# Reordering an attention block: four heads scored together, units by query tile, and a share of the normalisation on GpSimd

## The chip, the cores and the metric

The kernel runs on one core of a Trainium2 chip. Its time is the device time of one execution in microseconds (us); the median of several runs counts. TensorE (PE) multiplies matrices, and its weight loads have a row of their own (PEld). VectorE is DVE, ScalarE is ACT, GpSimd is POOL, and SyncE (SP) issues most transfers. Each engine works through its instructions in program order and waits for the others by semaphores. All data is float32.

## The reference, cut to what matters

The reference passes 8 sequences of 512 tokens with 128 features through four layers, each a half feed-forward, an attention and again a half feed-forward. Only the last layer, L3, is touched. It computes:

```
x = x + 0.5 * ffn(layernorm(x))
x = x + attention(layernorm(x))
x = x + 0.5 * ffn(layernorm(x))

attention:  q, k, v = x Wq' + bq, x Wk' + bk, x Wv' + bv     # 16 heads of 8 features
            s = q k' / sqrt(8)
            p = softmax(softmax(s))                          # twice
            h = p v
ffn:        probs = softmax(x gate'); the two largest of 8 experts are chosen
            y = sum over the two chosen of (x w_up[e]) w_down[e]
```

## The kernel before, in words

The kernel goes through the layers as blocks: L0, L1, L2 and, last, `l3_block` (L1212). The tensor `self.x[b]` of each of the 8 batches stays on the chip as four tiles of 128 tokens (128 partitions x 4 x 128).

**A unit of L3 attention.** A unit is a batch b, a group g of four heads and a tile i of 128 queries (L1316): 128 units, with i as the innermost index. The four heads of a group lie on four groups of 32 partitions, so that a score product uses a quarter of TensorE's rows. A unit goes through these steps:
- `score(n, h)` (L1238): for the head pair h, two products of 128 queries by 512 keys into one double bank of PSUM, tag `s1`, of which there are two.
- `maximum` (L1246): VectorE takes the negated row maximum of both heads (L1248).
- `soften` (L1250): two exponentials on ScalarE with the row sum (L1255).
- `norm` (L1258): the reciprocal of the sums and a multiply of each head's 128x512 probabilities; VectorE does it (L1268) but for the fourth head in every second unit, which ScalarE does (L1266).
- `turn` (L1270): four transposes a head on TensorE into a bank of tag `tp` (L1276), so that keys lie on the partitions.
- `again` (L1280): the second softmax's exponential out of that bank (L1284). No maximum is needed, as its input lies between 0 and 1.
- `weigh` (L1287): 16 products with the values into bank `o`; a column of ones in the values gives the second softmax's sum. After the last tile of a group ScalarE copies the bank out (L1301).
- `back` (L1304): four transposes, the reciprocal and the multiply of the second softmax, once per batch and group; after a batch's last group, VectorE adds the result to `self.x[b]` (L1314).

**The order.** L1341 to L1370 write the order of PE, ACT and DVE by hand: an iteration n issues pieces of unit n (scores, maxima, exponentials), n-1 (normalisation, turns, second exponential) and n-2 (`weigh`). The score of the first head pair is issued at the end of the iteration before, and the pairs stand apart from each other.

**Other work between the units.** `self.plan` puts steps of other work at given iterations into `todo`, and an iteration runs its list just before `weigh`. This work is, for each batch, the entry of the attention (`whiten`, the layer norm, with `measure` L160: VectorE's statistics, thirteen small GpSimd operations, then one GpSimd operation L197 per tile; `turned` L228: four transposes and a ScalarE copy; `project` L1704 twice and `values` L1718) and the closing feed-forward (`l3_ffn_steps` L266: whiten, turned, route, choose, choose_next, then eight `apply` steps, each a product for four experts and four updates of x on VectorE, L297). Each `project` writes its result to memory and reads it back by four transfers in another layout, all issued on SP. A product of this other work uses the same three `tp` banks as the turns. The last batch's feed-forward begins at iteration 131 and runs after all units; the store of x follows its last `apply`.

Of the kernel before, what the change touches and what calls it, by code (L numbers as in the profile page):

```python
# [108 lines left out]
class Net:  # L109
    def __init__(self, ctx, tc, a, x_in, out):  # L110
# [17 lines left out]
        self.brief = ctx.enter_context(tc.tile_pool(name="brief", bufs=2))  # L128
        self.front = ctx.enter_context(tc.tile_pool(name="front", bufs=2))
# [30 lines left out]
    def measure(self, srcs, bias=False):  # L160
# [3 lines left out]
        n = 4 * len(srcs)  # L164
        st = small.tile([P, n, 6], F32, tag=f"bst{n}", name="st")
        for k, src in enumerate(srcs):
            for i in range(4):
                nc.vector.bn_stats(st[:, 4 * k + i, :], src[:, i, :])  # L168

        sm, d, q, ve, r0, h, rs = (small.tile([P, n], F32, tag=f"b{t}{n}", name=t) for t in ("sm", "d", "q", "ve", "r0", "h", "rs"))  # L170
# [20 lines left out]
    def whiten(self, b, out=None, src=None):  # L191

        src = self.x[b] if src is None else src
        sm, rs = self.measure([src])
        xn = self.act.tile([P, 4, P], F32, tag="xn", name="xn") if out is None else out
        for i in range(4):
            self.nc.gpsimd.tensor_scalar(xn[:, i, :], src[:, i, :], sm[:, i : i + 1], rs[:, i : i + 1], ALU.subtract, ALU.mult)  # L197
        return xn
# [29 lines left out]
    def turned(self, xn, bank, out=None):  # L228

        nc = self.nc  # L230
        pt = bank("pt")
        for i in range(4):
            nc.tensor.transpose(pt[:, i * P : (i + 1) * P], xn[:, i, :], self.ident)
        xt = self.act.tile([P, 512], F32, tag="xt", name="xt") if out is None else out
        nc.scalar.copy(xt, pt)
        return xt

# [28 lines left out]
    def l3_ffn_steps(self, b, w, bank, done=None):  # L266
# [3 lines left out]
        box = {}  # L270

        def route(xt):
            lp = bank("lp", (P, 4, 8))
            for i in range(4):
                nc.tensor.matmul(lp[:, i, :], lhsT=xt[:, i * P : (i + 1) * P], rhs=gw, start=True, stop=True)
            box["steps"] = self.top2_steps(small, lp, 4, None, "b")
            return xt, box["steps"][0](None)
# [5 lines left out]
        def choose_next(got):  # L283
            xt, found = got
            _, o1, o2 = box["steps"][2](found)
            sel = small.tile([P, 4, 8], F32, tag="bsel", name="sel")
# [4 lines left out]
        def apply(got, i, h):  # L291
# [3 lines left out]
            for e in range(4):  # L295
                x = self.x[b][:, i, :]
                nc.vector.scalar_tensor_tensor(x, yp[:, e, :], sel[:, i, 4 * h + e : 4 * h + e + 1], x, ALU.mult, ALU.add)  # L297
            if done is not None and i == 3 and h == 1:
                done(b)
            return got  # L300

        experts = [lambda got, i=i, h=h: apply(got, i, h) for i in range(4) for h in range(2)]
        return [lambda _: self.whiten(b), lambda xn: self.turned(xn, bank), route, choose, choose_next] + experts

    def first_max(self, pool, v, n, tag, oh=None):

        nc = self.nc
        m = pool.tile([P, n], F32, tag=tag + "m", name=tag + "m")
        nc.vector.tensor_reduce(m, v, AX.X, ALU.max)
        r = pool.tile([P, n, 8], F32, tag=tag + "r", name=tag + "r")  # L310
        nc.vector.tensor_tensor(r, v, bc(m, 2, 8), ALU.is_equal)
        nc.vector.tensor_tensor(r, r, bc(self.const("rev"), 1, n), ALU.mult)
        f = pool.tile([P, n], F32, tag=tag + "f", name=tag + "f")
        nc.vector.tensor_reduce(f, r, AX.X, ALU.max)
        oh = pool.tile([P, n, 8], F32, tag=tag + "o", name=tag + "o") if oh is None else oh
# [3 lines left out]
    def top2_steps(self, pool, lp, n, bias, tag, to=(None, None, None)):  # L319
# [3 lines left out]
        def powers(_):  # L323
            lg = pool.tile([P, n, 8], F32, tag=tag + "lg", name="lg")
# [4 lines left out]
            m = pool.tile([P, n], F32, tag=tag + "lm", name="lm")  # L329
            nc.vector.tensor_reduce(m, lg, AX.X, ALU.max)  # L330
            nc.vector.tensor_tensor(lg, lg, bc(m, 2, 8), ALU.subtract)
            pr = pool.tile([P, n, 8], F32, tag=tag + "pr", name="pr") if to[0] is None else to[0]
# [3 lines left out]
        def largest(pr):  # L336
            s = pool.tile([P, n], F32, tag=tag + "ls", name="ls")
# [5 lines left out]
        def next_largest(got):  # L343
            pr, o1 = got
            p2 = pool.tile([P, n, 8], F32, tag=tag + "p2", name="p2")
# [866 lines left out]
    def l3_block(self, w2, w3, out):  # L1212
# [11 lines left out]
        with ExitStack() as c:  # L1224
# [6 lines left out]
            def bank(name, shape=(P, 512)):  # L1231
                return ps.tile(list(shape), F32, tag="tp", name=name, bufs=3)

            scores, maxima, rcs, probs, expos, outs, ats = {}, {}, {}, {}, {}, {}, {}

            def score(n, h):  # L1238
                b, g, i = units[n]
# [10 lines left out]
            def soften(n, h):  # L1250
                s, nm = scores.pop((n, h)), maxima.pop((n, h))
                sm = rcs[n, h] = wk.tile([P, 2], F32, tag="sm", name="sm", bufs=4)
                for jj in range(2):
                    e = wk.tile([P, 512], F32, tag="e", name="e", bufs=14)
# [3 lines left out]
            def norm(n, h):  # L1258

                rc = wk.tile([P, 2], F32, tag="rs", name="rs", bufs=4)  # L1260
                nc.vector.reciprocal(rc, rcs[n, h])
                rcs[n, h] = rc
                for jj in range(2):
                    e = probs[n][2 * h + jj]
                    if h and jj and n % 2:
                        nc.scalar.activation(e, e, AF.Copy, scale=rc[:, 1:2])  # L1266
                    else:
                        nc.vector.tensor_scalar(e, e, rc[:, jj : jj + 1], None, ALU.mult)  # L1268

            def turn(n, h):  # L1270

                banks = []
                for j in (2 * h, 2 * h + 1):
                    tp = bank("tp", (P, 4, P))
                    for kt in range(4):
                        nc.tensor.transpose(tp[:, kt, :], probs[n][j][:, kt * P : (kt + 1) * P], self.ident)  # L1276
                    banks.append(tp)
                return banks

            def again(n, banks):  # L1280

                for tp in banks:
                    p = wk.tile([P, 4, P], F32, tag="p2", name="p2", bufs=10)
                    nc.scalar.activation(p, tp, AF.Exp)  # L1284
                    expos.setdefault(n, []).append(p)

            def weigh(n):  # L1287
                b, g, i = units[n]
                if i == 0:
                    outs[b, g] = ps.tile([P, 512], F32, tag="o", name="o")  # L1290
                    if g == 0:
                        ats[b] = wk.tile([P, 4, P], F32, tag="at", name="at")
                o, p2 = outs[b, g], expos.pop(n)
                for kt in range(4):
                    for j in range(4):
                        nc.tensor.matmul(  # L1296
                            o[32 * j : 32 * j + 32, i * P : (i + 1) * P], lhsT=vas[b % 2][:, kt, 4 * g + j, :], rhs=p2[j][:, kt, :],
                            start=(kt == 0), stop=(kt == 3))
                if i == 3:
                    os = wk.tile([P, 512], F32, tag="os", name="os")  # L1300
                    nc.scalar.copy(os, o)  # L1301
                    outs[b, g] = os

            def back(b, g):  # L1304
                os = outs.pop((b, g))
                tp = bank("tp", (P, 4, 4, 32))
                for i in range(4):
                    nc.tensor.transpose(tp[:, i].rearrange("p j r -> p (j r)"), os[:, i * P : (i + 1) * P], self.ident)
                rc = wk.tile([P, 4, 4], F32, tag="rc", name="rc")
                nc.vector.reciprocal(rc, tp[:, :, :, 8])  # L1310
                nc.vector.tensor_tensor(
                    ats[b][:, :, 32 * g : 32 * g + 32].rearrange("p i (j d) -> p i j d", d=8), tp[:, :, :, 0:8], bc(rc, 3, 8), ALU.mult)
                if g == 3:
                    nc.vector.tensor_tensor(self.x[b], self.x[b], ats[b], ALU.add)  # L1314

            units = [(b, g, i) for b in range(NB) for g in range(4) for i in range(4)]  # L1316
# [8 lines left out]

            self.plan(todo, (0, 2, 3), *self.l2_ffn_steps(NB - 1, w2, bank))
            self.plan(todo, (4, *range(6, 18)), *self.l3_ffn_steps(NB - 1, w3, bank))
            for b in range(NB):
                if b:
                    n = 16 * b - 10  # L1330
                    self.plan(todo, (n, n + 2, n + 3, n + 4, n + 5), lambda _, b=b: self.whiten(b), lambda xn: self.turned(xn, bank, self.longer()),
                              lambda xt, b=b: l3.project(b, 0, xt, bank), lambda xt, b=b: l3.project(b, 1, xt, bank),
                              lambda xt, b=b: l3.values(b, xt, bank))
                for g in range(4):
                    also(16 * b + 4 * g + 6, back, b, g)
                n = 16 * b + 19
                self.plan(todo, (n, *range(n + 2, n + 14)), *self.l3_ffn_steps(b, w3, bank, store))
# [3 lines left out]
            with tc.manual_schedule(engines={mybir.EngineType.PE, mybir.EngineType.Activation, mybir.EngineType.DVE}):  # L1341
                for n in range(last + 20):
                    here, prev, two = 0 <= n < last, 0 <= n - 1 < last, 0 <= n - 2 < last
                    if n == 0:
                        score(0, 0)
                    if prev:
                        banks = turn(n - 1, 0)
                        again(n - 1, banks)
                    if here:
                        maximum(n, 0)  # L1350
                        score(n, 1)
                        soften(n, 0)
                    if prev:
                        norm(n - 1, 1)
                    if here:
                        maximum(n, 1)
                    for work in todo.pop(n, ()):
                        work()
                    if two:
                        weigh(n - 2)  # L1360
                    if prev:
                        banks = turn(n - 1, 1)
                    if here:
                        soften(n, 1)
                    if prev:
                        again(n - 1, banks)
                    if here:
                        norm(n, 0)
                        if n + 1 < last:
# [439 lines left out]
```

## Time and profile before

| | |
|---|---|
| median of 3 runs | 2884.49 us (2880.66 to 2885.62) |
| the profiled execution | 2895.91 us, its span 2894.1 us |
| busy: PE, DVE, ACT, POOL | 2610.5, 1920.7, 1738.7, 904.5 us |
| mean granted TensorE clock | 0.935 of full speed |
| L3: first score to the end | 2054.8 to 2894.1 us |
| last score of L3 | 2850.0 us |
| last exponential of the first softmax | 2852.6 us |

The busy time of an engine counts compute instructions only. A row of a group of instructions names the line, the engine, the operation, what is written and read, the shapes, the count, the busy time in total and the mean duration of one in ns, and last the idle time of the engine just ahead of it with what ended it. A float32 product appears as two matmul records, a transpose as one.

### The profile page before, as it was taken

What the parts mean: (1) busy time and instruction counts of PE and PEld (TensorE: products, weight loads), DVE (VectorE), ACT (ScalarE), POOL (GpSimd) and SP (SyncE); (2) the same over time, 40 slices, a digit from 0 to 9 for tenths busy, and PEclk for the clock granted to TensorE, in tenths of its full rate; (3) what the DMA queues carried; (4) which work ended last, traced back from release to release, by engine and by line L of the source; (5) the groups of instructions that cost most, each with busy time, mean ns of one, the idle gap of its engine ahead of it and who ended that gap; (6) DMA issues with size and microseconds to landing.
All of it is one profiled execution on the core that took longest, in us unless ns stands there. A gap on an engine that the chain in (4) does not pass through costs nothing.

```text
span 2894.1 us, 50615 instructions
## 1 busy us (share of the span) xinstructions
PE 2610.5 (90%) x18466; PEld 1504.0 (52%) x18466; DVE 1920.7 (66%) x5193; ACT 1738.7 (60%) x4258; POOL 904.5 (31%) x1907
## 2 busy tenths in 40 slices
PE   5857766999999998899999999999999999999997
PEld 4545543333333434565655656656555555555553
DVE  5336435788888763546566575654688888888886
ACT  2233133255555555666657566675588888888884
POOL 5744564122223231342524525323312201210200
PEclk9877775799999988999999999999899999999998
DMA  7120340000000000000000000000000000000000
GB/s 250 48 73 16 85 114 16 17 17 17 17 17 17 17 2 32 1 1 1 1 1 1 1 1 1 1 1 15 1 16 16 5 20 16 20 5 20 16 5 8
DMA packets 74343, 67.29 MB, mean 23 GB/s; under 512 B 17760, under 2 KB 63848, under 8 KB 71880
## 3 DMA queue, kind: packets, MB, share of 16 engines
q1 hardware_dynamic: 66128, 51.44, 6.6%
q0 software_dynamic: 3872, 8.11, 1.0%
q10 hardware_dynamic: 4096, 4.51, 0.5%
q8 instruction: 147, 2.41, 0.3%
q14 instruction: 100, 0.82, 0.1%
HBM read 36.74 MB, written 27.33 MB: 22 GB/s over the span
## 4 chain that ended last, share of the span: by engine, by line
PE 65%; DVE 13%; ACT 9%; POOL 8%; issue 3%; DMA 2%; SPq 0%; ACTq 0%; POOLq 0%; DVEq 0%
PE s L1244 8%; PE tp L1276 8%; PE s L1094 5%; PE o L1124 4%; PE o L1538 4%; PE yp L294 4%; PE o L1296 4%; PE s L1489 3%; DVE nm L1095 3%; PE tp L1515 3%; ACT e L1496 3%; PE pp L1458 2%; PE s L1114 2%; PE op L1552 2%; PE vp L1471 2%
## 5 line engine op out<-in xcount | busy, mean ns | idle before, releaser
L171 POOL TENSOR_TENSOR d<-st 128x4 f32<-128x4 f32 (+1 forms) x96 | 19.7, 205 | 1269.2 <-DVE st L168 666.2
L1248 DVE TENSOR_REDUCE nm<-s 128x2 f32<-128x1024 f32 x256 | 313.0, 1223 | 105.4 <-PE s L1244 105.0
L1095 DVE TENSOR_REDUCE nm<-s 128x2 f32<-128x1024 f32 x256 | 307.1, 1219 | 97.4 <-PE s L1114 84.6
L1255 ACT ACTIVATE e<-s,nm 128x512 f32<-128x512 f32 x512 | 351.0, 703 | 29.4 <-DVE nm L1248 29.4
L1116 ACT ACTIVATE pr<-s 128x512 f32<-128x512 f32 x512 | 274.5, 598 | 153.0 <-PE s L1114 144.9
L1114 PE MATMUL s<-q,k 32*128 32x512 f32 x1024 | 312.2, 644 | 10.7 <-ACT pr L1116 6.9
L1284 ACT ACTIVATE p<-tp 128x512 f32<-128x512 f32 x512 | 275.6, 609 | 72.1 <-PE tp L1276 69.9
L1094 PE MATMUL s<-k,q 32*128 32x512 f32 x1024 | 291.0, 672 | 19.0 <-DVE nm L1095 16.3
L1244 PE MATMUL s<-k,q 32*128 32x512 f32 x1024 | 292.0, 648 | 4.8 <-ACT e L1255 2.4
L1276 PE MATMUL tp<-cst,e 128*128 128x128 f32 x2048 | 287.0, 282 | 7.3 <-DVE e L1268 6.2
L1276 PEld LDWEIGHTS tp<-cst,e 128*128 128x128 f32 x2048 | 220.7, 142 | 138.4 <-issue 100.8
L1496 ACT ACTIVATE e<-e,m 128x512 f32<-128x512 f32 (+3 forms) x512 | 285.4, 567 | 7.7 <-DVE m L1493 7.5
L1493 DVE CUSTOM_DVE_ANT_0 e<-s,bias 128x512 f32<-128x512 f32 (+3 forms) x512 | 219.9, 486 | 98.9 <-PE s L1489 98.5
L1517 ACT COPY pt<-tp 128x512 f32<-128x512 f32 x320 | 173.9, 588 | 100.3 <-PE tp L1515 99.8
L1268 DVE TENSOR_SCALAR e<-e,rs 128x512 f32<-128x512 f32 x448 | 201.8, 487 | 9.1
L297 DVE SCALAR_TENSOR_TENSOR x<-yp,sel,x 128x128 f32<-128x128 f32 x512 | 178.5, 349 | 22.6 <-PE yp L294 8.2
L197 POOL TENSOR_SCALAR xn<-x,sm,rs 128x128 f32<-128x128 f32 x228 | 186.0, 827 | 6.1
L1489 PE MATMUL s<-qk 64*128 64x512 f32 (+3 forms) x1024 | 172.7, 456 | 2.3 <-DVE m L1493 1.6
L1515 PE MATMUL tp<-cst,e 128*128 128x128 f32 x1280 | 169.5, 279 | 1.7 <-ACT e L1496 1.7
L1515 PEld LDWEIGHTS tp<-cst,e 128*128 128x128 f32 x1280 | 141.7, 143 | 41.6 <-issue 16.4
L1546 DVE TENSOR_TENSOR att<-o,rt 128x512 f32<-128x512 f32 x64 | 44.3, 692 | 174.7 <-ACT rt L1545 174.7
L1524 POOL COPY rb<-rc 128x512 f32<-128x512 f32 x64 | 39.1, 611 | 383.9 <-DVE rc L1522 311.0
(394 smaller groups left out, 4904.2 us busy)
## 6 DMA issues: line engine op xcount, KB each, us to landing
yd<-z SPq DMA_DIRECT2D x8, 1024.0 KB
r<-yd SPq DMA_DIRECT2D x32, 256.0 KB
xd<-xn SPq DMA_DIRECT2D x16, 256.0 KB
k<-sk SPq DMA_DIRECT2D x64, 64.0 KB
sk<-pu SPq DMA_DIRECT2D x16, 256.0 KB
w<-in_l_w SPq DMA_DIRECT2D x14, 256.0 KB
q<-sq SPq DMA_DIRECT2D x32, 72.0 KB
x<-in_x SPq DMA_DIRECT2D x8, 256.0 KB
```

What stands on the lines that cost most here:

```text
L1094: nc.tensor.matmul(s[:, jj, :], lhsT=q[cut, g, i * P : (i + 1) * P], rhs=k[cut, g, :], start=True, stop=True)
L1095: nc.vector.tensor_reduce(nms[b, g // 2][:, i, 2 * h : 2 * h + 2, g % 2], s, AX.X, ALU.max, negate=True)
L1114: nc.tensor.matmul(s, lhsT=k[cut, g, kt * P : (kt + 1) * P], rhs=q[cut, g, :], start=True, stop=True)
L1116: nc.scalar.activation(e, s, AF.Exp)
L1244: nc.tensor.matmul(s[:, jj, :], lhsT=q[cut, g, i * P : (i + 1) * P], rhs=k[cut, g, :], start=True, stop=True)
L1248: nc.vector.tensor_reduce(nm, scores[n, h], AX.X, ALU.max, negate=True)
L1255: nc.scalar.activation(e, s[:, jj, :], AF.Exp, bias=nm[:, jj : jj + 1], accum_out=sm[:, jj : jj + 1])
L1276: nc.tensor.transpose(tp[:, kt, :], probs[n][j][:, kt * P : (kt + 1) * P], self.ident)
L1284: nc.scalar.activation(p, tp, AF.Exp)
L1489: nc.tensor.matmul(s[:, jj, 0:w], lhsT=qs[n][cut, i * P : (i + 1) * P], rhs=ks[n][cut, 0:w], start=True, stop=True)
L1496: outs.append(lambda e=e, jj=jj: nc.scalar.activation(e, e, AF.Exp, bias=mins[n][:, jj, i : i + 1], scale=-1.0, accum_out=sums[n][:, jj, i ...
L1515: nc.tensor.transpose(tp[:, k, :], block(n, jj, i, kt), self.ident)
```

## The change

1. A unit is now (b, i, g): the head group is the innermost index, so that one query tile is complete after four units. `back` works on one tile for all 16 heads and GpSimd adds it to that tile of x.
2. Both score pairs are issued together at the head of the iteration. Turns move later: heads 0 and 1 of unit n-1 are turned at the end of iteration n, heads 2 and 3 at the head of iteration n+1, between the second exponentials of heads 0 and 1, in two `tp` banks.
3. Other products have one bank of their own, tag `w`; after the last unit, the two double banks of the scores.
4. ScalarE normalises no more; GpSimd normalises the fourth head of each unit from unit 14 on.
5. ScalarE operations of the other work are collected in `self.late` and issued after `soften(n, 0)` or at the end of the iteration. The transfers of `project` are put off with them. The router's exponential is not collected.
6. Other work has new iterations, some in a second place (n + 0.5) after `weigh`; whitening goes tile by tile; GpSimd, too, is in the order written by hand.
7. The last batch's feed-forward is done for tiles 0 to 2 and for tile 3 separately, the first from iteration 127 on.
8. `e` has 12 buffers for 14, `p2` 8 for 10. The helpers take fewer than four tiles.

```diff
@@ turned, scalar
-        xt = self.act.tile([P, 512], F32, tag="xt", name="xt") if out is None else out
-        nc.scalar.copy(xt, pt)
+        xt = self.act.tile([P, 512], F32, tag="xt", name="xt")[:, 0 : n * P] if out is None else out
+        self.scalar(xt, pt, AF.Copy)
         return xt
+
+    def scalar(self, *args, **kwargs):
+
+        work = lambda: self.nc.scalar.activation(*args, **kwargs)
+        if self.late is None:
+            work()
+        else:
+            self.late.append(work)
@@ l3_block
-                return ps.tile(list(shape), F32, tag="tp", name=name, bufs=3)
+                n = int(np.prod(shape[1:]))
+                t = ps.tile([P, 512] if spare[0]["tag"] == "w" else [P, 1024], F32, name=name, **spare[0])[:, 0:n]
+                return t if len(shape) == 2 else t.rearrange("p (a b) -> p a b", b=shape[2])
+
+            turned, spare = dict(tag="tp", bufs=2), [dict(tag="w", bufs=1)]
...
-                    if h and jj and n % 2:
-                        nc.scalar.activation(e, e, AF.Copy, scale=rc[:, 1:2])
-                    else:
-                        nc.vector.tensor_scalar(e, e, rc[:, jj : jj + 1], None, ALU.mult)
...
+                    (nc.gpsimd if h and jj and n >= 14 else nc.vector).tensor_scalar(e, e, rc[:, jj : jj + 1], None, ALU.mult)
+
+            def turn(n, j):
+
+                tp = ps.tile([P, 4, P], F32, name="tp", **turned)
+                for kt in range(4):
+                    nc.tensor.transpose(tp[:, kt, :], probs[n][j][:, kt * P : (kt + 1) * P], self.ident)
+                turns.setdefault(n, []).append(tp)
...
+            def back(b, i):
+                os = outs.pop((b, i))
+                tp = bank("tp", (P, 16, 32))
+                for g in range(4):
+                    nc.tensor.transpose(tp[:, 4 * g : 4 * g + 4].rearrange("p j r -> p (j r)"), os[:, g * P : (g + 1) * P], self.ident)
+                rc, at = wk.tile([P, 16], F32, tag="rc", name="rc"), wk.tile([P, 16, 8], F32, tag="at", name="at")
+                nc.vector.reciprocal(rc, tp[:, :, 8])
+                nc.vector.tensor_tensor(at, tp[:, :, 0:8], bc(rc, 2, 8), ALU.mult)
+                x = self.x[b][:, i, :]
+                nc.gpsimd.tensor_tensor(x, x, at.rearrange("p h d -> p (h d)"), ALU.add)
+
+            units = [(b, i, g) for b in range(NB) for i in range(4) for g in range(4)]
...
             self.plan(todo, (0, 2, 3), *self.l2_ffn_steps(NB - 1, w2, bank))
-            self.plan(todo, (4, *range(6, 18)), *self.l3_ffn_steps(NB - 1, w3, bank))
+            self.plan(todo, (6, 7, 8, 9, 10, 12, 13, 14, 14.5, 15, 16, 17, 19, 20, 21, 22.5, 25.5), *whiten(NB - 1), *self.l3_ffn_steps(NB - 1, w3, bank)[1:])
             for b in range(NB):
+                n = 16 * b
                 if b:
-                    n = 16 * b - 10
-                    self.plan(todo, (n, n + 2, n + 3, n + 4, n + 5), lambda _, b=b: self.whiten(b), lambda xn: self.turned(xn, bank, self.longer()),
+                    m = max(n - 20, 1)
+                    self.plan(todo, (m, m + 1, m + 2, m + 3, m + 4, n - 9, n - 7.5, n - 5, n - 4.5), *whiten(b), lambda xn: self.turned(xn, bank, self.longer()),
                               lambda xt, b=b: l3.project(b, 0, xt, bank), lambda xt, b=b: l3.project(b, 1, xt, bank),
                               lambda xt, b=b: l3.values(b, xt, bank))
...
+                for i in range(4):
+                    also(n + 4 * i + 6, back, b, i)
+                if b < NB - 1:
+                    last_ones = (23, 24, 24.5, 25, 25, 27, 28, 29, 31, 32, 32.5, 33)
+                    self.plan(todo, [n + k for k in (19, 20, 21, 22, 23, *(last_ones if b == NB - 2 else (24, 25, 26, 27, 28, 29, 31, 32, 33, 35, 36, 37)))],
+                              *whiten(b), *self.l3_ffn_steps(b, w3, bank, store)[1:])
+                else:
+                    self.plan(todo, (n + 19, n + 20, n + 20.5, n + 21, n + 21.5, n + 22, n + 22.5), *self.l3_ffn_steps(b, w3, bank, store, (3, 4)))
+                    self.plan(todo, [n + k for k in (15, 16.5, 17, 17.5, 18, 19, 19.5, 20, 20.5, 20.5, 21)], *self.l3_ffn_steps(b, w3, bank, None, (0, 3)))
...
-            with tc.manual_schedule(engines={mybir.EngineType.PE, mybir.EngineType.Activation, mybir.EngineType.DVE}):
+            with tc.manual_schedule(engines={*FIXED, mybir.EngineType.Pool}):
                 for n in range(last + 20):
                     here, prev, two = 0 <= n < last, 0 <= n - 1 < last, 0 <= n - 2 < last
...
+                    if n == last:
+                        spare[0] = dict(tag="s1", bufs=2)
+                    if here:
+                        score(n, 0)
+                        score(n, 1)
+                    if two:
+                        for j in range(4):
+                            again(n - 2)
+                            if j < 2:
+                                turn(n - 2, 2 + j)
                     if here:
                         maximum(n, 0)
...
+                        maximum(n, 1)
                     if prev:
                         norm(n - 1, 1)
+                    works(n)
                     if here:
...
+                        soften(n, 0)
+                    put_off()
                     if two:
                         weigh(n - 2)
+                    works(n + 0.5)
                     if prev:
...
+                        turn(n - 1, 0)
+                        turn(n - 1, 1)
                     if here:
                         soften(n, 1)
...
                         norm(n, 0)
...
+                    put_off()
                 assert not todo
```

## The prediction

> **What bounds the kernel now.** I read the times first: the profiled execution took 2895.91 us (span 2894.1), 0.4% above the 2884.49 us median, so a sum made against it is scaled by 0.9961 at the end. Only the L3 block (2054.8 us to the end) changes. A table of busy time by stretch (us, then busy time of PE, PEld, DVE, ACT, POOL, then the granted clock) shows its limit:
>
> ```profile
> 2400.00:2500.00 100.00, 99.25 (x961) 57.65 (x958) 84.38 (x191) 86.18 (x210) 15.29 (x38) 1.00 0.06 15
> 2850.00:2894.00 44.00, 25.50 (x160) 12.67 (x156) 22.80 (x74) 8.17 (x19) 6.43 (x17) 0.78 0.04 12
> ```
>
> TensorE is full at full clock, here as in every hundred from 2100 to 2800; VectorE and ScalarE are at 85%. The groups of 2100 to 2840 us say how long a unit takes and of what it is made:
>
> ```profile
> L1255 ACT ACTIVATE e<-s,nm 128x512 f32<-128x512 f32 x475 | 325.7, 703 | 11.2 <-DVE nm L1248 11.2
> L1248 DVE TENSOR_REDUCE nm<-s 128x2 f32<-128x1024 f32 x238 | 291.0, 1223 | 90.2 <-PE s L1244 89.8
> L1244 PE MATMUL s<-k,q 32*128 32x512 f32 x952 | 268.2, 640 | 0.0
> L1284 ACT ACTIVATE p<-tp 128x512 f32<-128x512 f32 x476 | 256.0, 609 | 62.9 <-PE tp L1276 60.9 <-ACT p L1284 0.3
> L1268 DVE TENSOR_SCALAR e<-e,rs 128x512 f32<-128x512 f32 x417 | 187.8, 487 | 8.5
> L197 POOL TENSOR_SCALAR xn<-x,sm,rs 128x128 f32<-128x128 f32 x56 | 48.6, 878 | 1.5
> ```
>
> 952 score records are 119 units of 8 in 740 us: 6.22 us a unit, 99.5 us for a batch of 16. The other engines wait for PE, which waits for nearly nothing. From first to last score (2054.8 to 2850.0) 127 intervals take 795 us, 6.26 each.
>
> **Four heads at once.** Do four row groups run together? L1 attention answers: there `first` and `second` use complementary pairs of row groups.
>
> ```profile
> 928.77 0.70 PE L1094 MATMUL s<-k,q 32*128 32x512 f32 x2
> 928.79 0.70 PE L1114 MATMUL s<-q,k 32*128 32x512 f32 x2
> 929.31 0.59 PE L1094 MATMUL s<-k,q 32*128 32x512 f32 x2
> 929.32 0.59 PE L1114 MATMUL s<-q,k 32*128 32x512 f32 x2
> 929.85 0.48 PE L981 MATMUL pa<-par,ot 128*128 128x256 f32 x1
> ```
>
> Eight records (four heads) pass in 1.08 us, as four (two heads) do in L3: 1.06 us from one score to the next instruction. Against this stands the Trainium skill, "TensorE: Matmul & The Clock Gate", Part 3 (row/col tiling), which measured 3.07x for four row tiles, not 4x: four heads would take 4/3.07 = 1.30 of one pass, 1.38 us. By the rule the loop below is 0.32 us a unit longer, 41 us in all; I follow the row.
>
> PE thus loses 1.06 us a unit: a batch falls from 99.0 us (its busy time in most hundreds) to 82.0 us of PE, 5.13 a unit. VectorE loses eight of 56 normalisations (8 x 0.44 at their pace of 0.88 a pair) and L1314 (0.69): 84.9 (likewise) to 80.7, 5.04. ScalarE loses the eight copies of L1266 (0.758 each in its row): 86.2 to 80.2, 5.01. All would allow about 5.1 us.
>
> **What is late next: a loop through ScalarE and PE.** PE and ACT are in order. In the new loop both scores head the iteration, and the second needs the bank that the last exp of the unit before reads. Behind it on PE stand the turns of heads 2 and 3 of unit n-2, and ACT's third `again` waits for those. Durations:
>
> ```profile
> 2058.30 0.68 ACT L1255 ACTIVATE e<-s,nm 128x512 f32<-128x512 f32 x1
> 2059.12 0.50 PEld L1244 LDWEIGHTS s<-k,q 32*128 32x128 f32 x4 [3.66 <-ACT e L1255]
> ...
> 2854.07 1.06 PE L1276 MATMUL tp<-cst,e 128*128 128x128 f32 x8 [0.38 <-DVE e L1268]
> 2854.80 0.60 ACT L1284 ACTIVATE p<-tp 128x512 f32<-128x512 f32 x1 [0.42 <-PE tp L1276]
> ```
>
> Last exp to score 0.82; score to turn 1.06; turn to `again` 0.70 (0.69 to 0.73); two `again` 0.97; three further exps to the last, 3 x 0.665. Sum 5.55 us. So the period cannot be below 5.55, though no engine needs over 5.13. That the score pairs start apart (the first only needs PE, ready about 0.6 earlier) changes nothing: the second pair is on the loop.
>
> Beside the loop PE has 0.6 us to spare. VectorE's own round is 2.4 (maxima) + 0.68 (one normalisation) + 1.07 (two) = 4.15 plus the unit's other work, 1.4 without delay and up to about 1 more held over.
>
> **Other work, per batch.** Each unit gets one piece, which must pass the single bank `w`:
> - Activations put off to behind `soften(n, 0)` sit in the loop: two copies at 0.6 and one projection at 0.69: 1.9. Those behind `soften(n, 1)` fall in ACT's 0.95 us gap before the third `again`: 0.
> - Twice a batch two pieces meet in one unit (turned and first projection; second projection and values). The later product waits for the bank until ACT has read it, so PE reaches the next scores 0.7 late: 1.4.
> - The router's exp (L333) isn't put off. It stands on ACT ahead of `soften(n, 0)` and waits for VectorE's maxima, a normalisation and three small operations. It ends about 4.6 us after the score where `soften` could start at 2.73: 1.9. Now it waits 0.3.
> - VectorE units above 1.4: expert pieces (4 x 0.38 = 1.52), statistics with an expert piece (0.87 + 1.52), top-2 with a `back` (2.35) or with values (2.5). Carried from unit to unit, 1.35.
> - Pool: 0.5, below.
> Sum 7.0 us a batch, 0.44 a unit: period 5.98. 127 x (6.26 - 5.98) = 36 us.
>
> **One head in four on Pool.** No row has a 128x512 multiply by one scalar. From below: L1524 copies 128x512 in 0.61; an add of two such tensors (L260) took 1.27. From above: L197, two scalars on 128x128, 0.878 in this stage, times four is 3.5. The skill ("GPSIMD Engine Reference", 4.1) puts elementwise work on VectorE and calls one-input work on Pool roughly line-rate, near the lower end; L197's slope (0.80 at 128 columns, 0.20 at 4) speaks for the upper. I take 2.0. Pool starts after the second maximum of iteration n, 4.2 us after the last exp, and the turn that needs it comes a period later plus 2.4: 3.6 us of cover. All of the range is free, except where a whitening's thirteen small operations (4 us) stand ahead: up to 1.1 twice a batch, 0.5 taken. Pool's load is 2.0 + 1.0 a unit.
>
> Moved at no cost: projections' DMAs go later on SP but four or more units ahead of need (25 us against some 8); the adds of `back` go to Pool behind its normalisation, 0.4; fewer `e` and `p2` buffers cover three and two units, as many as are alive.
>
> **Start and end.** In the first 14 units VectorE keeps four normalisations (0.44 more, but fewer pieces): no difference taken. PE starts cold as now (0.50 until 2075 us). Clock: PE's idle share rises to 14%, but matmuls per us rise too; stretches of L2 with PE at 88 to 90% mostly show 1.00. Nothing is charged.
> The chain's end, from the last statistics:
>
> ```profile
> 2862.54 0.88 DVE st L168 x4
> ...
> 2868.27 2.34 POOL xn L197 x3
> ...
> 2871.81 1.89 PE lp L275 x8
> ...
> 2878.32 0.36 DVE x L297
> ```
>
> From there 31.6 us pass: whitening four tiles, routing (8 products), top-2 (4.6), 32 expert updates (12.6), store (3.1). After: one tile. Three expert pieces of the other tiles (4.6) hide under its 6.3 us of statistics, small operations, one whitening and routing; then in VectorE's order 0.9 + 3.1 + 1.8 + 1.5 + 1.8 + 3.1, and the store 3.1: 21.6. Ahead of the statistics Pool's slower normalisation (+1.5) and a top-2 step (+1.3) stand against the smaller add and back: even, within 3. Gain 10.
>
> **Sum.** 2895.9 - 36 - 10 = 2850; times 0.9961: 2839 us.
>
> **Rivals.**
> 1. The pieces hide better than worked out: period 5.55, 127 x 0.71 = 90, with the end 100: 2785 us. For: at full speed VectorE and ScalarE have 9% left. Against: the router's exp is in ACT's order for all to read. Chance 0.23.
> 2. It doesn't do what it says: the second pair waits, PE's saved 1.06 us turns into waiting for ACT, and pieces collide more: period 6.15 to 6.25, only the end gained: about 2878. For: the loop takes nearly all of a period now. Against: each collision would have to cost twice what I counted. Chance 0.06, half of it within 0.2%.
> 3. Slower: Pool's normalisation is late. Iteration n's turn of head 3 waits for it, and everything in order behind. The period is then d + 1.9, d its duration: beyond 3.6 it shows, at 4.35 the whole gain is gone, at 5 the period is 6.9: 127 x 0.64 - 10 = +71, 2956 us. For: 3.5 is an upper row, VectorE and Pool work at once (L197's mean is 0.878 beside 0.785 at the quiet end), and its scalar form is unknown. Against: two scalars and two operations cost more than one. Chance 0.09, with a clock that falls below 0.97 included.
> The forecast, periods of 5.8 to 6.15 (2816 to 2861 us): 0.62.
>
> **Numbers.** Under 0.2% (6 us) no measurement of this kernel tells from no change. Faster: 0.62 + 0.23 + 0.03 = 0.88; same 0.03; slower 0.09. The range goes from rival 1 to just short of no change, which leaves out about 0.07 below and 0.11 above: 2785 to 2880.
>
> **What would show it.** Right: eight score records of one line in 1.1 us or two fours overlapping; PE busy 86 in 100 us at clock 1.00; PE's scores waiting for ACT e; ACT p waiting for PE tp nearly 1 us once a unit; ACT pr waiting about 2 us for DVE lg eight times; an end of about 31 us after the last exp instead of 41. Wrong: PE turns waiting for Pool (rival 3); VectorE above 95 in 100 us, its maxima and not ACT setting the period; score passes of 1.4 us; a granted clock of 0.9 in the steady stretch.

## The result, and the profile after

| | before | after |
|---|---|---|
| median of 4 runs | 2884.32 us (2880.66 to 2885.62) | 2862.44 us (2856.28 to 2865.00) |
| profiled execution, its span | 2895.91, 2894.1 us | 2861.59, 2859.8 us |
| first to last score of L3 | 795.2 us, 6.26 a unit | 761.9 us, 6.00 a unit |
| end after the last exponential | 41.5 us | 44.6 us |

The ratio is 0.9909 [0.9891, 0.9928]: faster by some 26 us (the two medians differ by 22) where 46 were forecast. The median lies 1 us beyond the forecast's own band (2816 to 2861), within the range. The steady stretch gave nearly what was forecast; the end lost 3 us where it was to gain 10. Here and below, "the last exponential" is that of the first softmax, and its time is its start.

The table by stretch of the changed kernel (start and end, then us and busy time of PE, PEld, DVE, ACT and POOL, the granted clock last but two):

```profile
2600.00:2700.00 100.00, 96.56 (x994) 60.52 (x996) 86.49 (x187) 83.72 (x210) 45.87 (x54) 1.00 0.08 19
2830.00:2860.00 30.00, 12.42 (x23) 4.41 (x23) 17.40 (x70) 1.00 (x4) 4.08 (x15) 0.73 0.06 17
```

TensorE is still busy for 96.6 us in 100, though the prediction said 86. What fills it is seen in the timeline, in the scores of units 59 and 60:

```profile
2401.80 1.79 PE L1260 MATMUL s<-k,q 32*128 32x512 f32 x8
...
2402.47 0.30 PEld L1260 LDWEIGHTS s<-k,q 32*128 32x128 f32 x4 [0.36 <-ACT e L1271]
...
2409.30 1.14 PE L1260 MATMUL s<-k,q 32*128 32x512 f32 x8
```

Eight score records take 1.14 us when both banks are free (last line; 11 of the 79 units from 33 to 111), but 1.8 us in most units and 2.3 to 3.4 in ten: the second pair's weights wait until the last exponential has left its bank, and two of the four row groups run meanwhile. Such a wait is a line of the weight load, not idle time of PE, and PE counts as busy. So a nearly full PE row here is no sign that TensorE sets the pace. The waits of 2100 to 2800 us (who waited, for whom, us in total, times, longest) say who does:

```profile
ACT p L1292 <- PE tp L1286: 97.2, 126, 1.8
...
PEld s L1260 <- ACT e L1271: 69.3, 182, 1.6
...
PE pt L237 <- POOL xn L1336: 3.7, 1, 3.7
```

ScalarE waits for the turns and TensorE for the exponentials: the loop of the prediction, closed. The groups of the same stretch:

```profile
L1264 DVE TENSOR_REDUCE nm<-s 128x2 f32<-128x1024 f32 x233 | 274.7, 1216 | 42.4 <-PE s L1260 40.6
...
L1280 POOL TENSOR_SCALAR e<-e,rs 128x512 f32<-128x512 f32 x110 | 196.4, 1785 | 331.0 <-DVE rs L1277 208.6 <-PE yp L308 76.0 <-PE tp L1313 24.1
L1280 DVE TENSOR_SCALAR e<-e,rs 128x512 f32<-128x512 f32 x356 | 180.5, 535 | 8.3
```

VectorE's wait for the scores fell to 40.6 us in 700 (before, 89.8 in 740). GpSimd's normalisation takes 1785 ns, with 331 us of idle time ahead of its 110. Nobody waits for a normalised head in this stretch. But GpSimd's new share shows once, in the last line of the list: at unit 119 the last tile of a whitening stands behind a normalisation in GpSimd's order, and TensorE waits 3.7 us for it. Units 119 and 120 take 8.66 and 9.01 us; in the kernel with all normalisation on VectorE (below), which has no such wait, they take 6.09 and 6.96, 4.6 us less.

The end went wrong. The timeline behind the last unit's last exponential, which starts at 2815.24:

```profile
2820.58 2.37 POOL L200 TENSOR_SCALAR xn<-x,sm,rs 128x128 f32<-128x128 f32 x3
...
2822.93 1.57 POOL L1280 TENSOR_SCALAR e<-e,rs 128x512 f32<-128x512 f32 x1
2823.00 0.48 PE L237 MATMUL pt<-cst,xn 128*128 128x128 f32 x1 [0.45 <-POOL xn L200]
...
2823.27 3.58 PE L1286 MATMUL tp<-cst,e 128*128 128x128 f32 x16
...
2827.75 1.51 DVE L310 SCALAR_TENSOR_TENSOR x<-yp,sel,x 128x128 f32<-128x128 f32 x4 [5.48 <-PE yp L308]
...
2833.81 0.28 DVE L170 BATCH_NORM_STATS2 st<-x 128x6 f32<-128x128 f32 x1
```

GpSimd is in written order too. The whitening of tiles 0 to 2 (thirteen small operations and three large ones, 2816.03 to 2822.95) stands ahead of the last unit's normalisation, whose reciprocal was ready at 2817.0. On TensorE the transposes of that whitening stand ahead of all four turns of the last unit (3.58 us from 2823.27), also of those of heads 0 and 1, which VectorE had normalised by 2817; and VectorE idles 5.48 us. The last tile's statistics come 18.6 us after the last exponential; before, it was 9.9.

### The profile page after: what moved, and what is told of

Same layout as the page of the kernel before. It is cut to its first block, busy times and chain, and to the rows that moved or that the text cites. A ratio compares the mean times of both kernels' runs of the same rounds, so it can differ in the third digit from the quotient of the medians.

```text
span 2859.8 us, 51609 instructions
## 1 busy us (share of the span) xinstructions
PE 2553.0 (89%) x18466; PEld 1501.9 (53%) x18466; DVE 1912.5 (67%) x5154; ACT 1696.7 (59%) x4196; POOL 1133.2 (40%) x2066
## 4 chain that ended last, share of the span: by engine, by line
PE 64%; DVE 13%; ACT 9%; POOL 8%; issue 4%; DMA 2%; SPq 0%; ACTq 0%; POOLq 0%; DVEq 0%
PE tp L1286 8%; PE s L1260 7%; PE s L1107 5%; PE o L1137 4%; PE o L1302 4%; PE o L1575 4%; PE s L1526 3%; DVE nm L1108 3%; PE yp L308 3%; PE tp L1552 3%; ACT e L1533 3%; PE pp L1495 2%; PE s L1127 2%; PE op L1589 2%; PE vp L1508 2%
## 5 line engine op out<-in xcount | busy, mean ns | idle before, releaser
L1108 DVE TENSOR_REDUCE nm<-s 128x2 f32<-128x1024 f32 x256 | 306.7, 1218 | 93.6 <-PE s L1127 81.0
L1292 ACT ACTIVATE p<-tp 128x512 f32<-128x512 f32 x512 | 281.8, 611 | 108.4 <-PE tp L1286 108.0
L1280 POOL TENSOR_SCALAR e<-e,rs 128x512 f32<-128x512 f32 x114 | 203.3, 1783 | 341.9 <-DVE rs L1277 212.5
L1264 DVE TENSOR_REDUCE nm<-s 128x2 f32<-128x1024 f32 x256 | 301.8, 1217 | 49.6 <-PE s L1260 46.2
L1107 PE MATMUL s<-k,q 32*128 32x512 f32 x1024 | 288.9, 668 | 20.0 <-DVE nm L1108 16.6
L173 POOL TENSOR_TENSOR d<-st 128x4 f32<-128x4 f32 (+2 forms) x97 | 20.0, 206 | 631.0 <-DVE st L170 600.9
L1260 PE MATMUL s<-k,q 32*128 32x512 f32 x1024 | 230.1, 649 | 16.0 <-ACT e L1271 13.2
L1302 PE MATMUL o<-p,va 128*32 128x128 f32 x4096 | 161.9, 279 | 0.8 <-ACT p L1292 0.2
```

Of the source, the lines that this page charges most:

```text
L1107: nc.tensor.matmul(s[:, jj, :], lhsT=q[cut, g, i * P : (i + 1) * P], rhs=k[cut, g, :], start=True, stop=True)
L1108: nc.vector.tensor_reduce(nms[b, g // 2][:, i, 2 * h : 2 * h + 2, g % 2], s, AX.X, ALU.max, negate=True)
L1260: nc.tensor.matmul(s[:, jj, :], lhsT=q[cut, g, i * P : (i + 1) * P], rhs=k[cut, g, :], start=True, stop=True)
L1264: nc.vector.tensor_reduce(nm, scores[n, h], AX.X, ALU.max, negate=True)
L1280: (nc.gpsimd if h and jj and n >= 14 else nc.vector).tensor_scalar(e, e, rc[:, jj : jj + 1], None, ALU.mult)
L1292: nc.scalar.activation(p, turns[n].pop(0), AF.Exp)
```

## The experiments

The theory after the result: (a) the loop through ScalarE and TensorE sets the period, and the router's exponential lengthens it; (b) the missing gain is the written order of GpSimd and TensorE at the end. The main rival: VectorE, at 86 in 100 us, sets the period. A table at the end of the section gives the units of most runs. Every kernel but the first is the changed one with the edit shown.

**The two kernels again.**

> The kernel before once more, unchanged, for a second profile of it. The forecast scaled its sum by 0.9961 as though the profiled execution were longer everywhere. If that is so, the stretch ahead of L3 is again about 2055 us and the L3 stretch again 795 us from first to last score. The rival: the 11.5 us by which that one profile lay above the median were an accident of one execution and lie mostly ahead of L3; then this profile starts L3 at about 2045 to 2050 us, its L3 stretch stays at 795 us (within 1), and its whole time comes out near 2884 us.

> The changed kernel once more, unchanged, as the reference for what follows. All theories: 2862 us, give or take 3; 762 us from first to last score (6.00 a unit), 44.6 us from the last exponential of the first softmax to the end.

Before: one run of 2883.77 us, span 2882.0, first score at 2043.2 (first profile: 2054.8), then 794.7 us to the last score and 41.5 us of end. The 12 us by which the first profile was longer lie ahead of L3 and belong to that execution. After: 2859.15 us, ratio 0.9904 [0.9884, 0.9925]; 763.6 us, then 44.6. Both stretches repeat within 2 us.

**The end put in order.** The last unit's fourth head goes back to VectorE, and the whitened tiles are turned, and then routed, a unit later.

```diff
-  ... (15, 16.5, 17, 17.5, 18, 19, 19.5, 20, 20.5, 20.5, 21) ...
+  ... (15, 17.5, 18, 19, 19, 19.5, 19.5, 20, 20.5, 20.5, 21) ...
...
-  (nc.gpsimd if h and jj and n >= 14 else nc.vector) ...
+  (nc.gpsimd if h and jj and 14 <= n < last - 1 else nc.vector) ...
```

> The end of the block alone: the last unit's fourth head is normalised on VectorE (it stood on GpSimd behind the whitening of tiles 0 to 2), and the transposes of that whitening are issued after the last weigh instead of ahead of the last turns. Theory (the order of GpSimd and TensorE at the end ate the expected 10 us): the time from the last exponential to the end falls from 44.6 to about 36 us, the whole by 8 us, the period stays at 6.00. Rival (the end is bound by VectorE's updates and the low TensorE clock, not by the order): less than 3 us. Another rival (nothing else can start there because the store waits): no change.

2852.9 us, 0.9884 [0.9862, 0.9906], 6.3 us under the changed kernel beside it; the end falls from 44.6 to 38.7, by 5.9 where 8 were expected. In its timeline VectorE's wait is down to 1.68 us and the statistics come 12.2 us after the last exponential (2814.05):

```profile
2826.29 0.29 DVE L170 BATCH_NORM_STATS2 st<-x 128x6 f32<-128x128 f32 x1
```

(b) holds for that part, for the two moves together; a later run, with all normalisation on VectorE, takes the first of them alone. From the statistics on nothing moved: 26.5 us, 26.0 in the changed kernel.

**The router's exponential put off like the other work.**

```diff
-  nc.scalar.activation(pr, lg, AF.Exp)
+  self.scalar(pr, lg, AF.Exp)
```

> One operation more is put off: the router's exponential goes behind soften(n, 0) like the other ScalarE work, instead of standing ahead of it and waiting for VectorE. Theory (the period is set by the loop through ScalarE and TensorE, and whatever stands in it adds its wait): 1.7 us less in nine units, 15 us in all, 2862 to about 2847, and the wait of pr for lg falls from 1.7 us each to nearly 0. Rival (VectorE sets the period, ScalarE's wait is slack): less than 3 us.

2845.8 us, 0.986 [0.9837, 0.9882]: 13 us under the changed kernel for 15 expected, 11 of them in the stretch (752.5 us). The operation now stands behind the exponential of the first head pair and waits 0.51 us, where it waited 1.84 (first line: the changed kernel):

```profile
2393.88 0.23 ACT L346 ACTIVATE pr<-lg 128x32 f32<-128x32 f32 x1 [1.84 <-DVE lg L344]
...
2384.72 0.23 ACT L244 ACTIVATE pr<-lg 128x32 f32<-128x32 f32 x1 [0.51 <-DVE lg L344]
```

(L244 is the helper `scalar`.) Only the unit that holds it and the next change by over 0.06 us (9 and 10 in the table): 1.3 and 0.8 us less than in the repeat. (a) holds.

**All normalisation on VectorE.**

```diff
-  (nc.gpsimd if h and jj and n >= 14 else nc.vector) ...
+  nc.vector ...
```

> The part with GpSimd undone: VectorE normalises all four heads of every unit, nothing else differs. Theory (VectorE has about 0.1 us a unit to spare beside the loop, and 0.44 more go over it): VectorE's round becomes 4.6 plus 1.3 of other work, the period rises to 6.15 to 6.25, the whole by 15 to 30 us. The end gets shorter by 2 to 6 us, as the last unit no longer waits for GpSimd. Rival A (VectorE is far from the limit): period unchanged, the whole 2 to 6 us faster. Rival B (VectorE sets the period already): +0.44 x 114 = 50 us.

2860.6 us, 0.9891 [0.9875, 0.9908]: not slower than the changed kernel by any measure of medians; the stretch is 770.3 us, 7 to 8 more, in a profiled execution that is the slowest of its four (2870.8). The expectation failed: 0.44 us more on VectorE hardly lengthened an ordinary unit (5.64 to 5.66 in places 0 to 6 of a batch), so VectorE had that much to spare there; places 9, 10 and 13 are clearly longer, 8.68, 7.17 and 5.99, the second of these with the clock at half speed in all five batches. GpSimd's share bought little.

Its end misses the expectation too: 45.4 us, no shorter than 44.6. The last unit's fourth head is now normalised on VectorE (first line), and its turns still come late, behind the transposes that wait for GpSimd's whitening:

```profile
2825.76 0.90 DVE L1280 TENSOR_SCALAR e<-e,rs 128x512 f32<-128x512 f32 x2
...
2831.82 0.33 PE L237 MATMUL pt<-cst,xn 128*128 128x128 f32 x1 [0.45 <-POOL xn L200]
2831.98 1.04 PE L1286 MATMUL tp<-cst,e 128*128 128x128 f32 x8
```

These turns start 8.4 us after the last exponential (2823.58), in the changed kernel 8.0, with the end put in order 5.3. So what held the end was the whitening's transposes in TensorE's order; taking the normalisation off GpSimd brought nothing while they stood there. Moving them alone was not run.

**The score pairs apart.** The second pair goes behind the first turns, as before the change; all else stays.

```diff
   score(n, 0)
-  score(n, 1)
   ... (the four second exponentials, turns of heads 2 and 3)
+  score(n, 1)
```

> The scoring of four heads together undone: the second pair is issued after the turns of heads 2 and 3 instead of right behind the first. Theory (four row groups overlap only while they are adjacent): TensorE's work a unit is again 5.1 + 1.06 = 6.2 us, it is busy 99 us in 100, the period is 6.2 to 6.3 and the whole 25 to 40 us slower than the changed kernel, that is at the time of the kernel before or slightly above. Rival (the overlap isn't what freed TensorE; the new order of the turns and the other work is): period within 0.05 of 6.00.

2930.38 us, 1.0136 [1.012, 1.0151]: slower than before. 6.22 us an ordinary unit (the median; 6.13 in the kernel before), 6.57 in the mean, and VectorE waits for the scores again (2100 to 2700):

```profile
DVE nm L1264 <- PE s L1260: 89.0, 96, 3.9
```

So the change needs the four heads scored together; without it the rest of the change costs 40 us (2890.5 before, beside it). The kernel is 71 us slower than the changed one, where 25 to 40 were expected for the lost overlap alone. The edit also puts the second pair, and with it its maximum and exponentials, behind the turns, and 51 us of this kernel's stretch pass at half clock; these parts were not separated.

**Fewer expert updates inside the units**, which takes VectorE's work away. The kernel leaves out three of four expert updates of L3, so its output lacks most of the last feed-forward; only its time is of use.

```diff
-  for e in range(4):
+  for e in range(4 if self.late is None else 1):
```

> Leaves out work: in L3 each expert step adds one of its four experts instead of all four, so the output lacks most of the feed-forward. VectorE loses 3 x 0.38 = 1.14 us in 72 expert steps, 82 us in all, some 6 of it after the last exponential. Theory (loop through ScalarE and TensorE; VectorE's work beside it only carries over now and then): the period falls from 6.00 by 0.05 to 0.15, 6 to 19 us, and the end by 5. Rival (VectorE sets the period): the period falls by 0.5 or more, at which ScalarE and TensorE would bind at 5.4.

2848.29 us, 0.9858 [0.9843, 0.9873]. All of the gain is the end (35.0 us), where the updates are left out too; the stretch is 762.5. VectorE's row fell from 516.7 to 475.1 busy us in 600 and it idled instead, 59.7 us for the scores (32.5 in the changed kernel) and, 2100 to 2700 (24.4 in the changed kernel):

```profile
DVE rs L1277 <- ACT e L1271: 45.6, 69, 1.6
```

The rival is out for the changed kernel.

**All mends together**, with two pieces of the attention's entry moved, so that no two share a unit:

```diff
   both edits above (end, router), and
-  ... n - 9, n - 7.5, n - 5, n - 4.5) ...
+  ... n - 9, n - 6.5, n - 5, n - 1.5) ...
```

> The mended end and the put-off router exponential together, and two pieces of other work moved so that no unit has two products waiting for the one bank: the first projection from n-7.5 to n-6.5, values from n-4.5 to n-1.5. Theory: the parts add: end 8, router's exponential 15, the two collisions 0.7 each for seven batches = 10: 33 us less than the changed kernel, about 2830; period 5.8. Rival (VectorE binds once the loop is shorter): period not below 5.9, the whole about 2845.

2838.55 us, 0.9829 [0.9812, 0.9845], the lowest median of a kernel that leaves nothing out, though not clear of the run without the move (below); stretch 752.4, end 38.4. That is 21 us under the changed kernel's repeat, where 33 were expected: in the stretch the moved pieces brought no more than the router's edit alone (752.5). Two further runs ask why: the same without the move, and the same with fewer updates (which again leaves out three of four).

> Keeps the tail order and the put-off router exponential of the version with all mends, but leaves the projection pieces at the iterations of the changed kernel, so that it tells what moving them was worth. If the collisions of two pieces in one bank are as cheap as the units of the mended version say (a batch 93.3 us there, 93.7 us with the exponential alone), the stretch from first to last score is 752 to 754 us, the end after the last exponential about 38.5 us, and the time within 0.2% of the mended version's: a ratio to the kernel before of 0.983 to 0.984. Rival: the collisions cost the 1.4 us a batch forecast and the move saved them; then it is 10 us slower, a ratio of 0.986 to 0.987.

> The version with all mends, with three of four expert updates of L3 left out inside the loop (so the result of the feed-forward lacks them). It asks whether VectorE sets the pace of the mended version. If TensorE and the loop do, the stretch from first to last score stays at 750 to 754 us and only the end falls, by up to 6 us (ratio 0.981 to 0.983). If VectorE does, at its 522.6 busy us in 600, the 37 us a 600 us stretch that are taken away shorten the stretch by 8 us or more (to 745 or less, ratio 0.978 or less).

Without the move: 2840.99 us, 0.9834 [0.9816, 0.9852]; stretch 751.0. With fewer updates: 2830.76 us, 0.9814 [0.9789, 0.9838]; stretch 747.6, end 31.7; the stretch lies between the two outcomes named beforehand (750 to 754, and 745 or less). The table has the reason: mean us a unit, from the start of one unit's last exponential to that of the next, over units 33 to 111, by place in the batch of 16 (unit 16 b + p is at place p; places 13 and 14, 5.6 to 5.7 in all of these, are left out).

| place | after | after again | end | router | without move | all mends | and fewer updates |
|---|---|---|---|---|---|---|---|
| 0 to 6 | 5.65 | 5.64 | 5.64 | 5.63 | 5.64 | 5.64 | 5.64 |
| 7, 8 | 6.11 | 6.11 | 6.11 | 6.11 | 6.11 | 6.11 | 6.11 |
| 9 | 8.33 | 8.33 | 8.33 | 7.01 | 7.01 | 5.75 | 5.75 |
| 10 | 6.02 | 6.41 | 6.43 | 5.59 | 5.59 | 6.19 | 6.19 |
| 11 | 6.26 | 6.24 | 6.24 | 6.19 | 6.19 | 6.18 | 6.18 |
| 12 | 6.33 | 6.32 | 6.32 | 6.27 | 6.27 | 5.69 | 5.69 |
| 15 | 5.61 | 5.61 | 5.61 | 5.62 | 5.61 | 6.53 | 6.06 |
| batch | 95.62 | 95.95 | 95.96 | 93.71 | 93.75 | 93.28 | 92.81 |

The first projection, whose delay moves from place 9 to 10, takes 1.26 off the one and puts 0.60 on the other: 0.66 us was the collision and 0.60 the piece itself, if the piece costs the same in both. The values product, moved from 12 to 15, takes 0.58 off and puts 0.92 on. With fewer updates 0.47 of that is gone, so there VectorE is late as well. With places 13 and 14 the net is -0.47 a batch, for the five batches here: a piece without company still has a price of about 0.6. The stretch doesn't show even this, because units 1 to 32, which the table leaves out, are 3.6 us longer in all with the move than without (6.08 a unit for 5.97).

## Where the prediction held and where it failed

**The sum.** Forecast: 36 in the stretch and 10 at the end. Measured against the repeated kernel before, whose L3 has no accident ahead of it: 794.7 - 761.9 = 32.8 in the stretch; 1.6 lost between last score and last exponential (2.6 us before, 4.2 after); 3.1 lost at the end. That is 28.1; the ratio says 26 and the two medians 22. The first score of L3 alone comes at 2042 to 2057 us in the profiled executions, so the stretches are the firmer figures. The scale of 0.9961 took 11 us off; the excess of the first profile proved to be 12 us, all ahead of L3, so it did no harm.

**Four heads at once: right, with its size in busy time wrong.** Eight records take 1.14 us; none of the 79 units takes the 1.38 worked out from the 3.07x of the Trainium skill ("TensorE: Matmul & The Clock Gate", Part 3). For this shape and type the measurement decides against that figure: four row groups take the time of two (1.13 us for the four records of one pair before). But "PE loses 1.06 us a unit" (5.13) was off: 96.6 busy us in 100 are 5.8 a unit, as the pairs start 0.67 apart. I had seen that they start apart and had still counted them as one pass.

**The loop: right.** 5.63 us in ordinary units for 5.55 worked out, and ScalarE's wait for the turns and TensorE's for the exponentials in the lists. Pairs apart (6.22) and fewer updates (no change) confirm it from both sides.

**Other work: right in sum, mixed in its terms.** Forecast 7.0 us a batch over 16 x 5.55, so 95.8; measured 95.62, which is 5.5 over 16 x 5.63. That the sums agree is in part luck: two terms of 1.9 together (VectorE's carry and GpSimd) were not there, while the ordinary unit was 0.08 longer, 1.3 a batch. The router's exponential: 1.9 forecast; putting it off brought 1.9 (first profile) to 2.2 (repeat), of it 1.3 in its own unit and the rest in the next, where the clock fell (below); so the operation itself cost less than forecast, and the clock, charged at nothing, made up the difference. Collisions: 0.7 each forecast, 0.66 measured for the one that could be read. VectorE's carry: 1.35 forecast; taking its updates away brought nothing in the changed kernel (95.98 a batch, 95.95 in the repeat), so that term was not there. ScalarE's `pr` waited 13.7 us in 8, 1.7 each, for about 2 forecast.

**GpSimd's normalisation in the steady stretch: right but for one place.** 1.79 us for the 2.0 taken, between bounds of 0.61 and 3.5; no turn waits for it, as 3.6 us of cover said. It is three times the 0.61 us of the copy, so the Trainium skill's "roughly line-rate" ("GPSIMD Engine Reference", 4.1), which had spoken for the lower bound, does not hold for this multiply. Rival 3 is out. Not free was what the normalisation pushes back in GpSimd's order: a whitening, 4.6 us at units 119 and 120. That this is near the 0.5 a batch charged for the reverse case, a normalisation behind a whitening, is luck.

**The end: the step that failed.** The prediction put the part ahead of the statistics at "even, within 3" and the part from there at 21.6. Measured: 9.9 became 18.6 (+8.7), and 31.6 became 26.0 (-5.6). For the first I charged GpSimd's slower normalisation (1.5) and a top-2 step (1.3) but not the whole whitening that the written orders put ahead: on GpSimd ahead of the normalisation, and on TensorE, by its transposes, ahead of all the last turns. The same prediction had charged this in the steady stretch ("thirteen small operations stand ahead"), where there is cover; in the last unit there is none. The end put in order leaves 12.2 there: +2.3 for the 2.8 of those two charges. For the second part, "three expert pieces hide under 6.3 us of statistics, small operations, one whitening and routing" failed: in the timeline of the changed kernel VectorE's `lg` comes not 6.3 but 9.25 us after the statistics, since a product and an update of the other tiles stand ahead of the routing on TensorE and VectorE:

```profile
2839.53 2.07 PE L308 MATMUL yp<-wall,xt 128*128 128x512 f32 x2 [0.37 <-ACT xt L244]
...
2841.64 1.51 DVE L310 SCALAR_TENSOR_TENSOR x<-yp,sel,x 128x128 f32<-128x128 f32 x4 [4.51 <-PE yp L308]
2843.06 0.15 DVE L339 COPY lg<-lp 128x8 f32<-128x8 f32 x1
```

This second part was read from the trace only; no run puts the routing first, and TensorE's clock is at half speed from 2836.7 to 2846.9, whose share is unknown, so its 4.4 us stay argued. So do the 1.6 us ahead of the last exponential.

**The rivals.** Rival 1 (the pieces hide, 5.55) falls with places 7 to 12, rival 2 (6.15 to 6.25) with the period of 6.00. Its time was worked out wrongly: by the prediction's own sum these periods, with the end gained, give 2861 to 2873 us and not 2878. The measured time lies at the edge of that, by the lost end and not by the period.

## What to carry to other kernels

When an engine gets a new share of the work and a written order at once, follow its order, and that of the engines behind it, through the last unit, where nothing covers a wait: 3 us of loss stood there in place of 10 of gain. When two banks come free one after the other, a product that could run at once is spread over the gap, and the engine looks full while it waits; look at the weight load's waits before calling it the bound. An operation that waits for another engine (the router's exponential, 2 us a batch) is worth moving out of the loop; a piece that only takes its own time costs it in any place.

## What the runs showed of the hardware

**The clock in the loop.** The kernel before has no stretch below full clock between units 15 and 126. The changed one has stretches of 3.4 or 6.8 us at half speed, 10 us in the first profile and 17 in the repeat, three of these about 95 us apart (2295.8, 2391.3, 2486.9), each just behind the unit in which TensorE idles for the collision and the router's exponential. Place 10 shows their price in one and the same kernel: 5.6 us without one (5.9 in one batch), 6.4 and 6.9 with 3.4 us at half speed, 7.4 with 6.8. So 0.8 to 1.8 us each, some 4 us for the three of the repeat; the prediction had charged nothing. With the router's edit they are gone from that place. The remaining one of the repeat (2760.0, 3.4 us) comes with TensorE's 3.7 us wait at unit 119; the kernel with all normalisation on VectorE has neither. The kernel with pairs apart shows more of them (51 us in all), at TensorE busy 585 us in 600; what sets them off was not tested.

**Engines side by side.** VectorE's 128x512 multiply takes 535 ns in the mean, where it was 487 ns before the change. With all normalisation back on VectorE it is 500. Sorted by what GpSimd did at the same time (changed kernel, 2100 to 2700 us), it takes 482 ns beside nothing, 489 beside GpSimd's own normalisation (100 cases), but 541 beside a whitening alone (46), 692 beside the add of `back` alone (13) and about 800 where a normalisation meets one of the two (32). So the normalisation by itself is not what slows VectorE. On GpSimd the multiply by one scalar per partition takes 1785 ns for 512 columns, while two scalars take 0.8 us for 128 (0.79 at the quiet end, 0.95 in the mean of the stretch).
